# Attention's gates as tanh of half the projection, and new durations in the planner, in a two-layer kernel on one core

## The chip, the cores and the metric

The kernel runs on one core of one Trainium2 chip. The metric is the device time of one execution in microseconds (us), as the median of several runs. A separate execution was profiled; every view of the trace quoted here belongs to that one execution.

A core has five engines that run their own instruction streams in order and meet through semaphores: PE (TensorE, matrix products and transposes), DVE (VectorE), ACT (ScalarE, activation functions and copies), POOL (GpSimd) and SP, which here issues the DMA transfers. PEld in a profile is PE's loading of weights.

## The reference

Two layers work on an array `x` of 256 x 256 tokens with 128 channels, in float32. Only layer 0 matters for the change: attention along each of the 256 rows, with 4 heads of 32 channels, a mask, a bias that all rows share, and a gate.

```python
q = einsum('bnqc,hdc->bnhqd', q_x, wq) * scale
k = einsum('bnkc,hdc->bnhkd', kv_x, wk)
v = einsum('bnkc,hdc->bnhkd', kv_x, wv)
a = einsum('bnhqd,bnhkd->bnhqk', q, k) + mask_bias + triangle_bias
a = softmax(a, axis=-1)
o = einsum('bnhqk,bnhkd->bnhqd', a, v)
o = swapaxes(o, -2, -3)
g = sigmoid(einsum('bnqc,hdc->bnqhd', q_x, wg) + bg)
o = (o * g).reshape(...)
return einsum('bnqe,ce->bnqc', o, wo) + bo
...
x = x + attention(_gn(x), kv_x, ...)
x = x + layer_1(_gn(x), ...)
```

`_gn` normalises `x` by statistics over groups of channels. Layer 1 is a convolution, four selective scans over 65,536 tokens and an output product.

## The kernel before

`_layer0` works in two passes. The first reads all of `x` for its statistics. The second is attention: 64 groups of 4 rows, each row 256 tokens. `project(g)` lays out the work of a group, `row(i)` that of a row.

**No order is written by hand.** Each piece of work is a task with an engine (or a choice of two), a name in the table `COST` (L68 to L80: occupation and latency in us), a due time and the tasks that it needs. `Play` (L87) walks through model time: at each step it takes the task that can start first, and among those within `close` of it the one that is due first, and emits its instructions. Every engine then executes its stream in that order. So a number in `COST` is in no instruction, but it decides which instruction stands where, and which of two engines gets a copy.

**A group** (`project`). SP loads `xt`, `kt` and the mask `mk`. For each half `j` of the group's 1024 tokens, PE transposes four blocks of `xt` and of `kt` into PSUM (`tpx`, `tpk`); DVE normalises the first into `xn` (L62), ACT or DVE copies the second into `kvT` (L373). PE multiplies by `wq`, `wk`, `wv` (`pq`, `pk` at L451, `pv` at L475), and ACT or DVE takes the result out to `qT`, `kT`, `v`. The gate is the product `pg` (L495): two 512-column products, one for each half, held in two banks of PSUM at once until a single ACT task `sigmoid` (L506) takes out both with `AF.Sigmoid`, one instruction for each half, into `gT`.

**A row** (`row`). PE forms the scores `sp` of the four heads (L557, 16 matmuls of 32 x 128, four PSUM banks of their own), DVE adds the bias that POOL has put together (L538) and takes the row's extreme (L576, cost `soft`), ACT takes the exponential and its sum (L590, cost `exp2`, two instructions for each head), PE transposes the result (`pT`, L628), and ACT or DVE copies it out to `e` (L373). DVE inverts the sums (L610), POOL spreads them (`bc`, L615). PE then puts into one bank (`po`) two transposes of `bc` (L646) and 16 matmuls of `e` by `v` (L651, tiles of 128 x 32). DVE multiplies that by the gate and by the inverse sum (L659, L660) into `og`, PE multiplies by `wo` (`pout`, L674), and DVE adds the residual (L680). After each fourth row SP stores the group, and PE turns it (`x1p`) for the statistics of layer 1.

**PSUM** has eight banks: four for the scores, four (`banks`) for everything else. A job (`job`, L353) takes a bank when its PE work starts and gives it back when the engine that takes the result out is done.

A row's tasks are due by the row number `i`: scores at `i - 0.6`, exponentials and transposes of head `h` at `i + 0.6 + 0.2h`, `po` at `i + 1.5`, `pout` at `i + 2`. The gates' products were due at `U - 1`, with `U` the group's first row, and the sigmoid at `U - 2`.

The weights are turned once at the start (L266 to L273), each from PSUM to SBUF with an ACT copy. `vec["bg"]` holds the gate's bias as a column.

Of the kernel before, what the change touches and what calls it, by code (L numbers as in the profile page):

```python
# [8 lines left out]
F32 = mybir.dt.float32  # L9
AF = mybir.ActivationFunctionType  # L10
ALU = mybir.AluOpType
# [4 lines left out]
P = 128  # L16
N = 256
# [43 lines left out]
def _normalise(nc, out, in_, mr):  # L61
# [3 lines left out]
SEM = 0.07  # L65
# [9 lines left out]
    "turn8": (0.885, 1.05), "mm": (0.87, 1.05), "dp": (1.0, 1.15), "turn4": (0.45, 0.62),  # L75
    "turn_b": (0.67, 0.85), "dma": (0.36, 1.6), "dma2": (0.72, 3.2),
    "d512": (0.60, 0.69), "n512": (0.62, 0.81), "t256": (0.34, 0.42), "og": (0.76, 0.85),
    "soft": (0.85, 0.95), "exp2": (0.90, 1.0), "gate": (3.85, 2.60), "bias": (4.54, 4.55),
    "bc": (0.62, 0.70), "four": (0.95, 1.25), "dma3": (1.0, 1.6),
}  # L80


# [4 lines left out]
class Play:  # L87
# [14 lines left out]
    def task(self, eng, cost, due, emit, deps=(), gate=None, more=0, lag=0.0):  # L102

        t = Task()
        t.eng = (eng,) if isinstance(eng, str) else eng
        t.cost = (cost,) if isinstance(cost, str) else cost
        t.due, t.emit, t.gate, t.after, t.by = due, emit, gate, [], None
        t.ready, t.left, t.lag = 0.0, more, lag
        for d in deps:
            if d.by is None:  # L110
                d.after.append(t)
                t.left += 1
            else:
                t.ready = max(t.ready, self.after_own(d) if t.eng == (d.by,) else d.end + SEM)
        if t.left == 0:
            self.offer(t)
        return t
# [79 lines left out]
def free_after(tasks, then):  # L197
    count = Countdown(len(tasks), then)
    for t in tasks:
        on_done(t, count.one)  # L200
# [19 lines left out]
def both(*gates):  # L220
    gates = [g for g in gates if g is not None]

    def gate():
        latest = 0.0
        for g in gates:
            r = g()
            if r is None:
                return None
            latest = max(latest, r)
        return latest  # L230

    return gate


def _layer0(tc, ctx, const, ident, gmat, vec, a, x1, x1T):


    nc = tc.nc
# [3 lines left out]
    BPG = RG * NB  # L242
    W = RG * N

    keep = ctx.enter_context(tc.tile_pool(name="l0keep", bufs=1))
    wk = ctx.enter_context(tc.tile_pool(name="l0wk", bufs=1))
# [18 lines left out]
    wT = {}  # L265
    for w in ("wq", "wk", "wv", "wg", "wo"):  # L266
        raw = wk.tile([P, C], F32, tag=f"raw_{w}", name=f"raw_{w}")
        src = a[f"L0_conv_{w}"]
        nc.sync.dma_start(raw, src if w == "wo" else src.rearrange("h d c -> (h d) c"))
        pt = any_bank.tile([P, 512], F32, "m", f"pt_{w}")  # L270
        nc.tensor.transpose(pt[:, 0:P], raw, ident)
        wT[w] = keep.tile([P, P], F32, tag=w, name=f"{w}T")
        nc.scalar.copy(wT[w], pt[:, 0:P])  # L273
    bo = keep.tile([P, 1, C], F32, tag="bo", name="bo")
    nc.sync.dma_start(bo[:, 0, :], a["L0_conv_bo"].partition_broadcast(P))
    tri = keep.tile([P, NB, H, N], F32, tag="tri", name="tri")
# [7 lines left out]
    scale = 1.0 / float(CH) ** 0.5  # L284
# [99 lines left out]
    def cols(j):  # L384
        return slice(j * 512, (j + 1) * 512)
# [27 lines left out]
    def project(g):  # L413

        U = RG * g
        w = groups[g] = {
            k: Lazy(k, f"{k}_{g}")
            for k in ("xt", "kt", "mk", "xn", "kvT", "qT", "kT", "gT", "v", "x1t", "x1c")
        }

        def load(kind, src):
            def emit(t):
                nc.sync.dma_start(w[kind].get().rearrange("p (t c) -> p t c", c=C), tokens(src, g))

            return emit

        def load_mask(t):
            src = a["L0_conv_mask_bias"][0, g * RG : (g + 1) * RG, 0, 0, :]
            nc.sync.dma_start(
                w["mk"].get().rearrange("p (r k) -> p r k", k=N), src.partition_broadcast(P)  # L430
            )

        lx = sp(U - 8, load("xt", x), (), w["xt"].gate)
        lk = sp(U - 8, load("kt", kv), (), w["kt"].gate)
        w["masked"] = sp(U - 7, load_mask, (), w["mk"].gate)
        xn, kvT, q, k, v, gates = [], [], [], [], [], []
        for j in range(BPG // 4):
            xn.append(job(
                f"tpx_{g}_{j}", U - 5 + j, [("turn4", turned(lambda: w["xt"].tile, j))],
                lambda pt, by, j=j: _normalise(nc, w["xn"].tile[:, cols(j)], pt, mr0), [lx], "n512",  # L440
                "DVE", w["xn"].gate, w["xn"].get,
            ))
            kvT.append(job(
                f"tpk_{g}_{j}", U - 5 + j, [("turn4", turned(lambda: w["kt"].tile, j))],
                copy(lambda j=j: w["kvT"].tile[:, cols(j)]), [lk], gate=w["kvT"].gate,
                first=w["kvT"].get, **EITHER,
            ))
        for j in range(BPG // 4):

            def product(what, src, j=j):  # L450
                return lambda pt: nc.tensor.matmul(  # L451
                    pt, wT[what], w[src].tile[:, cols(j)], start=True, stop=True
                )

            def scaled(pt, by, j=j):
                dst = w["qT"].tile[:, cols(j)]
                if by == "ACT":
                    nc.scalar.mul(dst, pt, scale)
                else:
                    nc.vector.tensor_scalar(dst, pt, scale, None, ALU.mult)  # L460

            q.append(job(
                f"pq_{g}_{j}", U - 4.5 + j, [("mm", product("wq", "xn"))], scaled, [xn[j]],
                gate=w["qT"].gate, first=w["qT"].get, **EITHER,
            ))
            k.append(job(
                f"pk_{g}_{j}", U - 2.4 + j, [("mm", product("wk", "kvT"))],
                copy(lambda j=j: w["kT"].tile[:, cols(j)]), [kvT[j]], gate=w["kT"].gate,
                first=w["kT"].get, **EITHER,
            ))  # L470

            def values(pt, j=j):
                for i in range(4):
                    t = 4 * j + i
                    nc.tensor.matmul(  # L475
                        pt[:, i * P : (i + 1) * P], w["kvT"].tile[:, t * P : (t + 1) * P], wT["wv"],
                        start=True, stop=True,
                    )

            v.append(job(  # L480
                f"pv_{g}_{j}", U - 2 + j, [("mm", values)],
                copy(lambda j=j: w["v"].tile[:, cols(j)]), [kvT[j]], gate=w["v"].gate,
                first=w["v"].get, **EITHER,
            ))
        free_after([kvT[0], kvT[1]], w["kt"].free)
        free_after([*k, *v], w["kvT"].free)

        held_banks = {}

        def gate_of(j):  # L490
            def emit(t):
                w["gT"].get()
                at = banks.take()
                held_banks[j] = (at, ps.tile([P, 512], F32, tag=f"m{at}", name=f"pg_{g}_{j}"))
                nc.tensor.matmul(  # L495
                    held_banks[j][1], wT["wg"], w["xn"].tile[:, cols(j)], start=True, stop=True
                )

            return emit

        def two_banks():
            return banks.free[1][0] if len(banks.free) > 1 else None

        g0 = task("PE", "mm", U - 1, gate_of(0), xn, both(two_banks, w["gT"].gate))
        g1 = task("PE", "mm", U - 1, gate_of(1), [g0], banks.gate)

        def sigmoid(t):
            for j in range(BPG // 4):
                nc.scalar.activation(
                    w["gT"].tile[:, cols(j)], held_banks[j][1], AF.Sigmoid, bias=vec["bg"]  # L510
                )
                banks.give(held_banks[j][0], t.end + SEM)

        gated = task("ACT", "gate", U - 2, sigmoid, [g0, g1])
        free_after([*q, g1], w["xn"].free)

        def add_bias(t):
            xt = w["xt"].tile.rearrange("p (t c) -> p t c", c=C)
            nc.gpsimd.tensor_tensor(xt, xt, bo.to_broadcast([P, BPG, C]), ALU.add)

        biased = task("POOL", "pool", U + 0.5, add_bias, xn)
        w.update(q=q, k=k, pv=v, gated=gated, biased=biased, ends=[])
        w["row"] = {
            kind: Countdown(RG, w[kind].free) for kind in ("mk", "qT", "kT", "gT", "v", "xt")
        }

    def row(i):
# [128 lines left out]

        def gate(pt, by):
            og = z["og"].get()
            nc.vector.tensor_tensor(og, pt[:, 0:N], w["gT"].tile[:, at], ALU.mult)  # L659
            nc.vector.tensor_tensor(og, og, pt[:, N : 2 * N], ALU.mult)  # L660

        og = job(
            f"po_{i}", i + 1.5, [("four", weigh)], gate, [*leaves, bc, w["gated"], *w["pv"]], "og",
            "DVE", z["og"].gate, None,
        )
        free_after([og], z["bc"].free)
# [1307 lines left out]
```

## Time and profile before

| what | value |
|---|---|
| median of 3 runs | 24744.65 us (24725.2 to 24746.45) |
| the profiled execution | 24753.32 us |
| its span, first to last instruction | 24751.6 us |
| mean granted TensorE clock | 0.982 |
| first scores of attention (L557) | 154.26 us after the span's start |
| first scores of the last row | 2040.45 us |
| busy over the whole span | PE 93%, DVE 95%, ACT 95%, POOL 94% |

Attention's second pass fills about 154 to 2050 us; layer 1 all that follows. The shares over the whole span are therefore those of layer 1 above all. The prediction goes by windows of attention alone.

How to read the lines of a profile that follow. A line such as `L495 PE MATMUL pg<-xn,wgT` names the line of the kernel, the engine, the operation and the tiles (written <- read). In a timeline the first number is the start in us from the span's start, the second the time from the first start to the last end of the instructions merged into the line, `x4` their number, and the bracket the engine's idle time just before them with what ended it. In the list of groups the numbers after `|` are busy us in all and the mean ns of one, and then the idle time before them. Matmuls are pipelined: the next can start before the shown end, so the distance between starts tells more than the length.

### The profile page before, as it was taken

How to read it: one execution, taken by the hardware profiler on the slowest of the kernel's cores; microseconds unless marked ns; L12 is line 12 of the kernel's file. 1: busy time of each engine (PE TensorE's matmuls, PEld its weight loads, DVE VectorE, ACT ScalarE, POOL GpSimd, SP SyncE). 2: the span in 40 equal slices, each digit the busy share in tenths (PEclk: the TensorE clock that was granted, in tenths of full speed). 3: DMA queues.
4: the chain of work that ended last, by engine and by line, in shares of the span. 5: the costliest groups of instructions: out<-in, count | busy, mean ns of one | idle time of the engine just before them, and what ended most of it. 6: DMA issues, size and time to landing. Idle time of an engine off the chain costs nothing. (4 is left out here: it accounts for less than half of the span.)

```text
span 24751.6 us, 464821 instructions
## 1 busy us (share of the span) xinstructions
PE 23003.9 (93%) x165172; PEld 18188.1 (73%) x165172; DVE 23434.1 (95%) x19272; ACT 23427.6 (95%) x46416; POOL 23325.3 (94%) x17424
## 2 busy tenths in 40 slices
PE   8999999999999999999999999999998888888888
PEld 6666666666666788888887777777777777777777
DVE  7887999999999999999999999999999999999999
ACT  7998899999998999999999999999999999999998
POOL 5777999999999999999999999999999999999999
PEclk9999999999999999999999999999999999999999
DMA  4225777777777666666666777777775555555555
GB/s 131 90 90 171 255 259 264 259 260 262 261 259 255 233 233 225 232 228 229 231 230 232 243 245 243 244 243 244 244 243 198 180 184 178 181 182 181 185 178 168
DMA packets 2471853, 5355.13 MB, mean 216 GB/s; under 512 B 177121, under 2 KB 1366424, under 8 KB 2469528
## 3 DMA queue, kind: packets, MB, share of 16 engines
q1 hardware_dynamic: 2469240, 5324.34, 64.0%
q8 instruction: 1305, 21.38, 0.4%
q14 instruction: 1020, 8.36, 0.1%
q0 software_dynamic: 288, 1.05, 0.0%
HBM read 4846.54 MB, written 478.15 MB: 215 GB/s over the span
## 5 line engine op out<-in xcount | busy, mean ns | idle before, releaser
L1805 POOL TENSOR_TENSOR hc<-w,c 128x1024 f32<-128x1024 f32 x6255 | 14726.7, 2376 | 529.5 <-DVE w L1787 195.1
L1787 DVE TENSOR_TENSOR_SCAN w<-w,hst,s 128x1024 f32<-128x1024 f32 x5550 | 12670.6, 2329 | 295.0 <-PE s L1741 143.8
L1824 PE MATMUL y<-ident,hc 128*128 128x128 f32 x65536 | 8478.1, 277 | 520.8 <-ACT part L1377 204.8
L1741 PE MATMUL s<-ident,bx 128*128 128x128 f32 x57344 | 7713.6, 279 | 1020.7 <-DVE w L1787 662.0
L1741 PEld LDWEIGHTS s<-ident,bx 128*128 128x128 f32 x57344 | 6428.1, 142 | 3009.5 <-DVE w L1787 1289.0
L1335 ACT ACTIVATE bx<-dtuT,bT 128x256 f32<-128x256 f32 x19751 | 8578.3, 502 | 2.8 <-PE s L1741 2.5
L1824 PEld LDWEIGHTS y<-ident,hc 128*128 128x128 f32 x65536 | 7445.2, 142 | 1407.1 <-POOL hc L1805 598.2
L1721 ACT ACTIVATE w<-dt,negA 128x1024 f32<-128x1024 f32 x7168 | 8126.5, 1148 | 31.3 <-PE y L1824 15.8
L1337 POOL TENSOR_SCALAR bx<-dtuT,bT 128x256 f32<-128x256 f32 x8921 | 4103.7, 483 | 22.6 <-ACT dtuT L1034 5.9
L1787 DVE TENSOR_TENSOR_SCAN s<-w,hst,s 128x1024 f32<-128x1024 f32 x1618 | 3775.7, 2338 | 310.1 <-PE s L1741 205.7
L1805 DVE TENSOR_TENSOR hc<-s,c 128x1024 f32<-128x1024 f32 x1937 | 2366.2, 1223 | 101.6 <-DVE s L1787 27.5
L1762 POOL TENSOR_TENSOR w<-xu,b 128x1024 f32<-128x1024 f32 x1024 | 2423.2, 2372 | 0.5 <-issue 0.4
L1093 PE MATMUL cv<-xn,wtap 128*128 128x512 f32 x4608 | 2217.6, 600 | 5.5 <-ACT xn L1080 5.5
L1787 DVE TENSOR_TENSOR_SCAN w<-s,hst,w 128x1024 f32<-128x1024 f32 x705 | 1642.3, 2337 | 58.8 <-ACT s L1721 55.1
L538 POOL TENSOR_TENSOR bias<-tri,mk 128x2048 f32<-128x2048 f32 x256 | 1167.1, 4559 | 378.8 <-DVE nm L576 218.2
L1812 ACT COPY hst<-w 128x1 f32<-128x1 f32 x6255 | 1138.1, 185 | 276.7 <-DVE w L1787 244.7
L1721 ACT ACTIVATE s<-dt,negA 128x1024 f32<-128x1024 f32 x1024 | 1143.0, 1116 | 89.1 <-DVE hc L1805 88.1
L1093 PEld LDWEIGHTS cv<-xn,wtap 128*128 128x128 f32 x4608 | 790.1, 193 | 529.4 <-issue 523.2
L1219 PE MATMUL dp<-xd,dtw 8*128 8x512 f32 x2048 | 1169.4, 662 | 5.2 <-ACT xd L1189 0.9
L590 ACT ACTIVATE s<-s,nm 128x256 f32<-128x256 f32 x2048 | 1028.3, 515 | 0.8
L576 DVE CUSTOM_DVE_ANT_0 s<-sp,bias 128x256 f32<-128x256 f32 x2048 | 754.4, 415 | 69.1 <-PE sp L557 61.1
L1787 DVE TENSOR_TENSOR_SCAN s<-s,hst,w 128x1024 f32<-128x1024 f32 x319 | 745.2, 2336 | 67.4 <-POOL w L1762 67.4
(183 smaller groups left out, 19594.3 us busy)
## 6 DMA issues: line engine op xcount, KB each, us to landing
c<-xp_d SPq DMA_DIRECT2D x7040, 512.0 KB
b<-xp_d SPq DMA_DIRECT2D x896, 512.0 KB
yrow_d<-ys SPq DMA_DIRECT2D x128, 1024.0 KB
yl<-yrow_d SPq DMA_DIRECT2D x512, 256.0 KB
xc_d<-xu SPq DMA_DIRECT2D x128, 512.0 KB
yl<-xc_d SPq DMA_DIRECT2D x128, 512.0 KB
xu<-xc_d SPq DMA_DIRECT2D x128, 512.0 KB
xcT_d<-wtap SPq DMA_DIRECT2D x128, 512.0 KB
```

What stands on the lines that cost most here:

```text
L538: nc.gpsimd.tensor_tensor(z["bias"].get(), tri.rearrange("p b h k -> p (b h) k"), w["mk"].tile.rearrange("p (r k) -> p r k", k=N)[:, r : r ...
L1093: return lambda pc: nc.tensor.matmul(pc, wtap[:, j, t, :], xn[:, 2 * q + u : 2 * q + u + 2, v : v + N], start=t == 0, stop=t == 8,)
L1219: return lambda pt: nc.tensor.matmul(pt, dtw[:, k, j, :], xd.half[0][0:R, q * 512 : (q + 1) * 512], start=True, stop=True,)
L1335: nc.scalar.mul(dst, src, b)
L1337: nc.gpsimd.tensor_scalar(dst, src, b, 1.0, ALU.mult, ALU.mult)
L1721: nc.scalar.activation(dst, w["dt"].half[j], AF.Exp, scale=negA[:, k * ND + j, n : n + 1])
L1741: nc.tensor.transpose(dst[:, x * P : (x + 1) * P], blocks(half)[:, x, :], ident)
L1762: nc.gpsimd.tensor_tensor(box["w"].half[0], w["xu"].half[j], b_now().half[0], ALU.mult)
L1787: nc.vector.tensor_tensor_scan(rev(states), rev(a), rev(b), hst[k][:, j, n : n + 1], ALU.mult, ALU.add)
L1805: eng.tensor_tensor(box["hc"].half[0], states, c_now().half[0], ALU.mult)
L1812: nc.scalar.copy(dst, src)
L1824: nc.tensor.matmul(gr["y"][:, x, :], hc[:, x * P : (x + 1) * P], ident, is_transpose=True, start=gr["fresh"] and x == 4 * q, stop=stop and ...
```

## The change

It has three parts.

The gate is computed as `sigmoid(y) = (1 + tanh(y / 2)) / 2`: ACT forms `tanh(0.5 * pg + 0.5 * bg)` with `AF.Tanh`; the multiplication on DVE becomes `(gT + 1) * po`; the factor of one half goes into `wo`, which is halved as it is copied.

The two halves of a gate become two ordinary jobs, due at `U - 2` and `U - 1`. Each holds one bank, and its own ACT instruction takes it out (cost `a512`).

Four durations of the planner change, and `weigh` gets a name of its own, `six`, where it shared `four` with the scores.

```diff
-    "soft": (0.85, 0.95), "exp2": (0.90, 1.0), "gate": (3.85, 2.60), "bias": (4.54, 4.55),
-    "bc": (0.62, 0.70), "four": (0.95, 1.25), "dma3": (1.0, 1.6),
+    "soft": (0.69, 0.79), "exp2": (0.985, 1.09), "gate": (3.85, 2.60), "bias": (4.54, 4.55),
+    "bc": (0.62, 0.70), "four": (1.07, 1.35), "six": (1.335, 1.6), "dma3": (1.0, 1.6),
...
-        nc.scalar.copy(wT[w], pt[:, 0:P])
+        nc.scalar.mul(wT[w], pt[:, 0:P], 0.5 if w == "wo" else 1.0)
+    hbg = keep.tile([P, 1], F32, tag="hbg", name="hbg")
+    nc.scalar.mul(hbg, vec["bg"], 0.5)
...
-        held_banks = {}
-
-        def gate_of(j):
-            def emit(t):
-                w["gT"].get()
-                at = banks.take()
-                held_banks[j] = (at, ps.tile([P, 512], F32, tag=f"m{at}", name=f"pg_{g}_{j}"))
-                nc.tensor.matmul(
-                    held_banks[j][1], wT["wg"], w["xn"].tile[:, cols(j)], start=True, stop=True
-                )
-
-            return emit
-
-        def two_banks():
-            return banks.free[1][0] if len(banks.free) > 1 else None
-
-        g0 = task("PE", "mm", U - 1, gate_of(0), xn, both(two_banks, w["gT"].gate))
-        g1 = task("PE", "mm", U - 1, gate_of(1), [g0], banks.gate)
-
-        def sigmoid(t):
-            for j in range(BPG // 4):
-                nc.scalar.activation(
-                    w["gT"].tile[:, cols(j)], held_banks[j][1], AF.Sigmoid, bias=vec["bg"]
-                )
-                banks.give(held_banks[j][0], t.end + SEM)
-
-        gated = task("ACT", "gate", U - 2, sigmoid, [g0, g1])
-        free_after([*q, g1], w["xn"].free)
+        gates = [
+            job(
+                f"pg_{g}_{j}", U - 2 + j, [("mm", product("wg", "xn", j))],
+                lambda pt, by, j=j: nc.scalar.activation(
+                    w["gT"].tile[:, cols(j)], pt, AF.Tanh, bias=hbg, scale=0.5
+                ), [xn[j]], "a512", gate=w["gT"].gate, first=w["gT"].get,
+            )
+            for j in range(BPG // 4)
+        ]
+        free_after([*q, *gates], w["xn"].free)
...
         def gate(pt, by):
             og = z["og"].get()
-            nc.vector.tensor_tensor(og, pt[:, 0:N], w["gT"].tile[:, at], ALU.mult)
+            nc.vector.scalar_tensor_tensor(
+                og, w["gT"].tile[:, at], 1.0, pt[:, 0:N], ALU.add, ALU.mult
+            )
             nc.vector.tensor_tensor(og, og, pt[:, N : 2 * N], ALU.mult)
...
-            f"po_{i}", i + 1.5, [("four", weigh)], gate, [*leaves, bc, w["gated"], *w["pv"]], "og",
+            f"po_{i}", i + 1.5, [("six", weigh)], gate, [*leaves, bc, *w["gates"], *w["pv"]], "og",
```

`product` moves out of the loop over `j` and takes `j` as an argument, so that the gates can use it. Layer 1 is not touched.

More of the change, by code (lines that the diff above doesn't have):

```diff
@@ L435, in project @@
         w["masked"] = sp(U - 7, load_mask, (), w["mk"].gate)
-        xn, kvT, q, k, v, gates = [], [], [], [], [], []
+        xn, kvT, q, k, v = [], [], [], [], []
         for j in range(BPG // 4):
@@ L447, in project, with product @@
             ))
+        def product(what, src, j):
+            return lambda pt: nc.tensor.matmul(
+                pt, wT[what], w[src].tile[:, cols(j)], start=True, stop=True
+            )
         for j in range(BPG // 4):
-            def product(what, src, j=j):
-                return lambda pt: nc.tensor.matmul(
-                    pt, wT[what], w[src].tile[:, cols(j)], start=True, stop=True
-                )
             def scaled(pt, by, j=j):
@@ L462, in project @@
             q.append(job(
-                f"pq_{g}_{j}", U - 4.5 + j, [("mm", product("wq", "xn"))], scaled, [xn[j]],
+                f"pq_{g}_{j}", U - 4.5 + j, [("mm", product("wq", "xn", j))], scaled, [xn[j]],
                 gate=w["qT"].gate, first=w["qT"].get, **EITHER,
@@ L466, in project @@
             k.append(job(
-                f"pk_{g}_{j}", U - 2.4 + j, [("mm", product("wk", "kvT"))],
+                f"pk_{g}_{j}", U - 2.4 + j, [("mm", product("wk", "kvT", j))],
                 copy(lambda j=j: w["kT"].tile[:, cols(j)]), [kvT[j]], gate=w["kT"].gate,
@@ L486, in project @@
         free_after([*k, *v], w["kvT"].free)
-        held_banks = {}
-        def gate_of(j):
-            def emit(t):
-                w["gT"].get()
-                at = banks.take()
-                held_banks[j] = (at, ps.tile([P, 512], F32, tag=f"m{at}", name=f"pg_{g}_{j}"))
-                nc.tensor.matmul(
-                    held_banks[j][1], wT["wg"], w["xn"].tile[:, cols(j)], start=True, stop=True
-                )
-            return emit
-        def two_banks():
-            return banks.free[1][0] if len(banks.free) > 1 else None
-        g0 = task("PE", "mm", U - 1, gate_of(0), xn, both(two_banks, w["gT"].gate))
-        g1 = task("PE", "mm", U - 1, gate_of(1), [g0], banks.gate)
-        def sigmoid(t):
-            for j in range(BPG // 4):
-                nc.scalar.activation(
-                    w["gT"].tile[:, cols(j)], held_banks[j][1], AF.Sigmoid, bias=vec["bg"]
-                )
-                banks.give(held_banks[j][0], t.end + SEM)
-        gated = task("ACT", "gate", U - 2, sigmoid, [g0, g1])
-        free_after([*q, g1], w["xn"].free)
+        gates = [
[8 more added lines that the diff above has]
+        free_after([*q, *gates], w["xn"].free)
         def add_bias(t):
@@ L521, in project @@
         biased = task("POOL", "pool", U + 0.5, add_bias, xn)
-        w.update(q=q, k=k, pv=v, gated=gated, biased=biased, ends=[])
+        w.update(q=q, k=k, pv=v, gates=gates, biased=biased, ends=[])
         w["row"] = {
@@ L658, in gate @@
             og = z["og"].get()
-            nc.vector.tensor_tensor(og, pt[:, 0:N], w["gT"].tile[:, at], ALU.mult)
+            nc.vector.scalar_tensor_tensor(
+                og, w["gT"].tile[:, at], 1.0, pt[:, 0:N], ALU.add, ALU.mult
+            )
             nc.vector.tensor_tensor(og, og, pt[:, N : 2 * N], ALU.mult)
         og = job(
-            f"po_{i}", i + 1.5, [("four", weigh)], gate, [*leaves, bc, w["gated"], *w["pv"]], "og",
+            f"po_{i}", i + 1.5, [("six", weigh)], gate, [*leaves, bc, *w["gates"], *w["pv"]], "og",
             "DVE", z["og"].gate, None,
```

## The prediction

> **What bounds the kernel now.** I read the table by stages first, because the page's shares mix attention with the 22.7 ms of layer 1, which the change leaves alone. The lines below are a steady stretch of attention; the columns are busy us of PE, PEld, DVE, ACT, POOL, then granted clock, DMA share, GB/s.
>
> ```profile
> 400.00:600.00 200.00, 196.24 (x1824) 138.85 (x1823) 165.49 (x625) 192.70 (x576) 148.00 (x62) 1.00 0.31 93
> 600.00:800.00 200.00, 195.61 (x1814) 137.65 (x1813) 165.36 (x624) 193.81 (x591) 148.18 (x61) 1.00 0.30 91
> ```
>
> Two engines are nearly full: PE 98%, ACT 96%. DVE (83%), POOL (74%) and DMA (30%) are not. Then the groups of ACT over the whole run:
>
> ```profile
> L509 ACT ACT_TABLE_LOAD x64 | 82.1, 1283 | 1.0
> L590 ACT ACT_TABLE_LOAD x64 | 82.1, 1283 | 1.2
> ```
>
> Each of the 64 groups of four rows loads the sigmoid's table and then the exponential's again: 2 x 1.283 = 2.57 us of ACT. The timeline of ACT around one gate shows where they stand:
>
> ```profile
> 624.12 1.28 ACT L509 ACT_TABLE_LOAD   x1
> 625.41 1.26 ACT L509 ACTIVATE gT<-pg,vecs 128x512 f32<-128x512 f32 x2
> 627.66 1.07 ACT L373 COPY e<-pT 128x512 f32<-128x512 f32 x2 [0.98 <-PE pT L628]
> 628.75 1.28 ACT L590 ACT_TABLE_LOAD   x1
> ```
>
> The load before this one for L590 began at 599.11, so a group takes 29.64 us. ACT itself waits 0.98 us for PE in it. So the loads are not simply the bound; what counts is what they cost PE. The timeline of PE, from the products before the first exponential of a group:
>
> ```profile
> 599.58 1.02 PE L451 MATMUL pk<-kvT,wkT 128*128 128x512 f32 x2
> 601.06 0.33 PE L628 MATMUL pT<-ident,s 128*128 128x128 f32 x1 [0.46 <-DVE x1t L680]
> 601.56 0.55 PE L628 MATMUL pT<-ident,s 128*128 128x128 f32 x3 [0.17 <-ACT s L590]
> 601.94 1.02 PE L451 MATMUL pq<-xn,wqT 128*128 128x512 f32 x2
> 602.80 0.60 PE L628 MATMUL pT<-ident,s 128*128 128x128 f32 x4
> 603.24 1.02 PE L451 MATMUL pk<-kvT,wkT 128*128 128x512 f32 x2
> 604.19 1.15 PE L557 MATMUL sp<-kT,qT 32*128 32x256 f32 x16
> 605.27 0.44 PE L646 MATMUL po<-ident,bc 128*128 128x128 f32 x2
> 605.64 1.07 PE L651 MATMUL po<-e,v 128*32 128x256 f32 x16
> 606.64 1.53 PE L628 MATMUL pT<-ident,s 128*128 128x128 f32 x12
> ```
>
> Here I take start to start, since modelled ends overlap. A 512-column product with undisturbed followers takes 0.86 (601.94 to 602.80), four transposes 0.44 (602.80 to 603.24). So pk at 599.58 could have been followed at 600.44; the next block starts at 601.06: 0.62 lost. That block of four then takes 0.88 to 601.94 instead of 0.44: 0.44 lost. Both losses stand on the exponential that came after the table load (599.11 to 600.39, first half 600.41 to 600.92). No other PE wait stands in the timeline of this group. **PE loses 1.06 us of 29.64 per group to the loads; the other 28.58 are PE's own work.**
>
> **A rule against this reading.** The Trainium skill (Trainium Kernel Development and Optimization, Performance Expectations) holds that PE's matmul busy time says little about the distance to its limit and that LDWEIGHTS busy time is to be taken. By that PE would be at 69% (138 of 200), ACT the only bound, and taking out 2.57 us of ACT per group would give 64 x 2.57 = 164 us. By the rows, PE's blocks repeat at the same interval in every group wherever no wait is shown (0.44, 0.86, 1.08), so PE streams without room. I follow the rows: the intervals, unlike busy time, are not modelled.
>
> **PE's own work per group, from start intervals.** 16 pT and 6 tpx, tpk, x1p at 0.4365 = 9.60; 4 po at 1.312 (610.66 to 611.97) = 5.25; 4 sp at 1.077 = 4.31; 6 pq, pk, pg at 0.8605 = 5.16; 2 pv at 0.893 (608.89 to 609.78) = 1.79; 4 pout at 0.446 = 1.78. Sum 27.89. On top come changes between tiled (sp and the e-times-v part of po) and whole-array matmuls: a block ahead of sp takes +0.093 (pk 603.24 to 604.19 is 0.95); a block of transposes after sp or po +0.057 (613.04 to 613.54 is 0.50; po after sp 605.27 to 606.64 is 1.37); a product after sp +0.10 (in the ramp, pq 155.33 to 156.29 is 0.96). Before: 3 x 0.093 + 7 x 0.057 = 0.68. 27.89 + 0.68 + 1.06 = 29.63, against 29.64 measured, so nothing is missing.
>
> **The change, part by part.**
>
> *Tanh for sigmoid.* Built, the changed program has 771 table loads; the trace of before has 898 in all. So 127 go, and tanh is served beside the exponential: one load remains in attention. Per group ACT loses 2.57 us. PE loses its 1.06 us of waiting, not 2.57: what is late next is PE's own stream. The Trainium skill (ScalarE: Activation LUTs, What ACT_TABLE_LOAD costs) prices a switch at about 2.66 us, a drain included; by it 127 x 2.66 = 338 us would go. The timeline shows 1.28 per load with the next instruction 0.01 to 0.02 later (624.12, 625.41), so no drain to be saved here; on ACT it is 127 x 1.283 = 163 us.
>
> *Each half on its way out.* Two activations of 128x512 per group as before (0.63 each, 1.26 for two), now apart, each freeing its own bank of PSUM. PE's pg products are as many as before. No trace row shows tanh: at best it costs a copy's 0.47 interval, at worst, by the nearest row (sigmoid), 0.63; I take 0.63. Either way ACT has room: in the built order ACT gets 20.05 copies a group (e 12.1, k and q 2 each, kv 2, v and x1c 1 each; 18.1 before) at 0.47 = 9.4, 32 exponentials at 0.49 = 15.7, two gates 1.3: 26.4 us of a group, 2.4 under PE's stream.
>
> *Gate multiply.* (tanh + 1) times po is one DVE instruction in place of one, 128x256. The nearest row is L659, 0.42 to 0.46; a multiply-add form could take up to twice that. DVE after: 16 soft x 0.69 = 11.0, 2 xn x 0.73 = 1.5, 6 copies x 0.60 = 3.6 (7.9 before), 4 og x 0.80 = 3.2, 4 residuals x 0.34 = 1.4, 4 reciprocals x 0.12, 2 statistics x 0.61 = 1.2: 22.4. Even 4 x 0.42 more leaves it 4.8 under PE. Nothing waits but pout, which stands at least two blocks of transposes behind its po.
>
> *Halves in the weights.* wo's copy becomes a multiply, and hbg is one 128x1 instruction more, once, before the ramp: 0.2 us at most, beside DMA waits of the first 128 us. A 4-byte tile more in SBUF: no cost.
>
> *New durations for the play.* They are in no instruction, but they reorder every engine. soft 0.69, exp2 0.985, sp 1.07 and po 1.335 are what the rows show (before: 0.85, 0.90, 0.95, 0.95), so waits of the plan should be waits of the chip. In the built order a steady group again has 42 PE blocks, the same work. But sp is now followed by pv, pout, pk and pT, never by po, and preceded by pT (twice), pout and tpk; every po is followed by pT. Changes of mode: 4 x 0.093 + 5 x 0.057 + 3 x 0.10 = 0.96, or 0.28 more than before. PE's stream is then 27.89 + 0.96 = 28.85. The Trainium skill (TensorEngine Tiling (Array Packing), Key Properties) says that a change of tiling mode drains TensorE; it speaks against this order, gives no price, and the rows above give it.
>
> *New waits.* SP's loads and stores keep number and size. With PE's running sum laid against ACT's and DVE's from a group's first sp: po of the second row starts at 12.0 and needs ACT's copy of its last pT (done in PE at 11.2; copy done near 12.0, needed at 12.4 after po's own transposes); pout of the third row, at 23.0, needs the bank of v's copy, which ACT gives near 22.9 to 23.0; the first pq at 4.6 needs xn near 4.4. All fit within 0.1 to 0.4 us. I allow 0.08 us a group, with 0 and 0.6 as ends: 0.6 if two of these miss by 0.3 each, behind which the whole PE stream stands.
>
> **Sum.** Group after 28.93, before 29.64: 0.71 less. From the first sp to that of the last group there are 63 periods: 45 us. Ramp and tail have the same work; I put them at nothing, plus or minus 4. Layer 1 has the same instructions in the same order on every engine. The profiled execution took 24753.3 (span 24751.6), so 24708; that execution lies 9 us above the median of the runs, 24744.65, so the forecast is **24,700**.
>
> **Rivals.** (1) *ACT was the bound*, PE stretches: 164 us less, 24,581. For it: ACT 96%, and the waits for "ACT s" by PE. Against it: the fixed intervals. 4%. (2) *The gain is eaten by new waits* at the places above: 0.4 to 0.8 us a group, leaving 0 to 25 us: about 24,732. For it: ACT's long unbroken run before them; against it: over 2 us of room a group. 27%. (3) *Slower, by PSUM banks*: the four banks of projections. Banks now also stand open for two gates until ACT comes round. If ACT reaches each gate or v late, the next PE block waits for the bank and the rest queues behind it. From 0.79 us a group on (29.64 less 28.85) it is slower; at 1.6, 0.8 per gate, 63 x 0.81 = 51 us: 24,796. Against it: the 2.4 us of room. 8%. (4) *Tanh in another table*: four loads a group, ACT 31.5: 63 x 1.9 = 120 us more, 24,865. The 771 loads exclude it nearly: 1%. The forecast has 60%.
>
> **How the numbers follow.** This kernel's measurement can tell about 0.2%, 49 us, from no change. The forecast's own ceiling is 63 x 0.79 = 50 us plus ramp and run scatter (the runs shown span 21 us); so of its 60%, 30 fall beyond 49 us and 30 within. With (1) faster has 34%; with (2) and a little of (3) within has 59%; slower 7%. The range, 24,668 to 24,747, takes the forecast with no wait, a cheaper change of modes (0.3 us a group, 19 us) and scatter at its low end, and (2) entire at its high end; (1), (3), (4) stay out.
>
> **What would show it.** Right: period near 28.9; no table load in a group; PE's pT after pk without the 0.62 and 0.44; PE near 99%, ACT near 91%; sp followed by a block lengthened by 0.06 to 0.10. Wrong: period under 28.8 (modes cheaper), or PE waits for ACT copies, xn or banks over 0.3 us a group; a gate multiply over 0.6 us; tanh over 0.7 us.

## The result and the profile after

| what | before | after |
|---|---|---|
| median of 7 runs each | 24743.59 us (24725.2 to 24751.1) | 24664.08 us (24656.99 to 24679.78) |
| span of the profiled execution | 24751.6 us | 24662.3 us |
| period of a group in attention | 29.64 us | 28.90 us |
| ACT's table loads in all | 898 | 771 |

The ratio of the times is 0.997, with a 95% interval of 0.9959 to 0.998: 79.5 us less. That is 34.5 us more than the 45 us forecast, 4 us below the low end of the range, and on the far side of 0.2%, where the prediction put its smaller chance.

The traces can be cut at four marks: the start of the first scores, the start of the last row's scores, the first scan of layer 1, and the end. The second column spans 255 rows.

| trace | to the first scores | first to last scores | to the first scan | layer 1 from there |
|---|---|---|---|---|
| before | 154.3 | 1886.2 | 100.0 | 22611.1 |
| after | 139.9 | 1832.7 | 102.2 | 22587.5 |
| difference | -14.4 | -53.5 | +2.2 | -23.6 |

The four sum to the 89.3 us between the two spans. Attention's share is 8.5 us above the forecast. The first column was forecast at nothing. Layer 1 has the same instructions in the same order; its share is taken up below.

The steady stretch of attention after, in the table by stages (columns as before: busy us of PE, PEld, DVE, ACT, POOL, then clock, DMA share, GB/s):

```profile
400.00:600.00 200.00, 200.00 (x1852) 142.61 (x1854) 160.60 (x628) 186.70 (x594) 151.41 (x64) 1.00 0.31 93
600.00:800.00 200.00, 200.00 (x1864) 142.94 (x1864) 159.87 (x621) 186.89 (x596) 153.82 (x63) 1.00 0.31 93
```

PE is covered without a gap, ACT has come down from 96% to 93%, DVE from 83% to 80%. The waits of the same stretch, longest first (who waited, for whom, us in total, times, longest):

```profile
POOL bias L523 <- DVE nm L561: 210.6, 152, 2.7
DVE s L561 <- PE sp L542: 127.3, 167, 1.5
POOL bias L523 <- PE pT L613: 121.6, 55, 2.5
ACT e L375 <- PE pT L613: 96.8, 111, 1.3
```

Before, the same list had two waits of PE's matmuls:

```profile
PE pT L628 <- ACT s L590: 20.0, 78, 0.5
PE pT L628 <- DVE x1t L680: 13.9, 30, 0.5
```

Now it has none; the other engines wait, mostly for PE. The timeline of PE shows what a group consists of:

```profile
602.30 0.60 PE L613 MATMUL pT<-ident,s 128*128 128x128 f32 x4
602.83 1.15 PE L542 MATMUL sp<-kT,qT 32*128 32x256 f32 x16
603.90 0.71 PE L661 MATMUL pout<-woT,og 128*128 128x128 f32 x4
604.45 0.60 PE L613 MATMUL pT<-ident,s 128*128 128x128 f32 x4
...
609.41 1.15 PE L542 MATMUL sp<-kT,qT 32*128 32x256 f32 x16
610.48 1.12 PE L452 MATMUL pk<-kvT,wkT 128*128 128x512 f32 x2
611.45 0.38 PE L631 MATMUL po<-ident,bc 128*128 128x128 f32 x2
...
622.53 1.15 PE L542 MATMUL sp<-kT,qT 32*128 32x256 f32 x16
623.61 1.16 PE L478 MATMUL pv<-wvT,kvT 128*128 128x128 f32 x8
624.60 1.02 PE L452 MATMUL pg<-xn,wgT 128*128 128x512 f32 x2
```

From start to start: the pT ahead of sp takes 0.53 in place of 0.44, pout after sp 0.55 in place of 0.45, pk after sp 0.97 in place of 0.86, pv after sp 0.99 in place of 0.89. They agree with the surcharges of 0.093 and 0.10 in the prediction's sum.

The costs of the two altered instructions, in the list of groups (busy us in all, mean ns of one, idle time before them). First before, then after for 300 to 1900 us:

```profile
L509 ACT ACTIVATE gT<-pg,vecs 128x512 f32<-128x512 f32 x128 | 81.0, 684 | 0.8
L659 DVE TENSOR_TENSOR og<-po,gT 128x256 f32<-128x256 f32 x216 | 90.8, 420 | 88.3 <-PE po L651 88.3
```

```profile
L494 ACT ACTIVATE gT<-pg,hbg 128x512 f32<-128x512 f32 x111 | 76.6, 690 | 3.7
L644 DVE SCALAR_TENSOR_TENSOR og<-gT,po 128x256 f32<-128x256 f32 x221 | 92.5, 418 | 74.3 <-PE po L636 74.3
```

Tanh takes 690 ns where the sigmoid took 684, and add-and-multiply 418 where the multiply took 420. Neither form costs anything that matters here.

### The profile page after: what moved, and what is told of

Read it like the earlier page. It is cut to its first block, busy times and chain, and to the rows that moved or that the text cites. A ratio compares the mean times of both kernels' runs of the same rounds, so it can differ in the third digit from the quotient of the medians.

```text
span 24662.3 us, 463909 instructions
## 1 busy us (share of the span) xinstructions
PE 22976.3 (93%) x165172; PEld 18190.0 (74%) x165172; DVE 23350.1 (95%) x19150; ACT 23324.4 (95%) x46412; POOL 23322.3 (95%) x17424
```

## The experiments

Every kernel was timed against the kernel before on the same chip. A period is the distance between the first scores of successive groups.

### Is the shorter statistics pass a matter of place?

The statistics pass has the same instructions on PE and DVE in the same order, but its loads of `x` came faster. The table by stages for that pass, first of before, then of after (last column: GB/s):

```profile
20.00:40.00 20.00, 11.51 (x88) 9.23 (x87) 13.32 (x21) 0.00 (x0) 0.00 (x0) 1.00 1.20 290
40.00:60.00 20.00, 11.74 (x89) 9.41 (x88) 14.66 (x24) 0.00 (x0) 0.00 (x0) 1.00 1.17 288
```

```profile
20.00:40.00 20.00, 13.25 (x101) 10.54 (x100) 16.44 (x26) 0.00 (x0) 0.00 (x0) 1.00 1.11 331
40.00:60.00 20.00, 12.87 (x98) 10.37 (x99) 15.60 (x25) 0.00 (x0) 0.00 (x0) 1.00 1.09 327
```

The 128x1 tile `hbg` takes 32 bytes of each partition in the layout, and everything behind it in layer 0 moves up. The first `xs` tile lies at byte 62688 before, an odd multiple of 32, and at 62720 after, a multiple of 64; the other `xs` tiles follow 4096 bytes apart. Two kernels tell place from chance.

**The tile alone** (before, with an unused tile where `hbg` would be):

```diff
+    pad = keep.tile([P, 1], F32, tag="pad", name="pad")
+    nc.scalar.mul(pad, vec["bg"], 0.5)
     bo = keep.tile([P, 1, C], F32, tag="bo", name="bo")
```

> The kernel before with one unused 128x1 tile at the place where the change puts hbg, so that the tiles behind it in SBUF move by 32 bytes, from an odd multiple of 32 to a multiple of 64. Theory A (the faster statistics pass of the profile after comes from where the tiles lie): the pass ends near 112 us instead of 126, the loads of x come each 1.51 us instead of 1.80, attention's period stays at 29.64, and the time falls by about 14 us. Rival B (chance of that execution): the pass ends near 126 us and the time is that of before.

**The change with the tiles at their old remainders:**

```diff
-    hbg = keep.tile([P, 1], F32, tag="hbg", name="hbg")
+    hbg = keep.tile([P, 16], F32, tag="hbg", name="hbg")[:, 0:1]
```

> The changed kernel with hbg's tile 64 bytes wide, so that the tiles behind it lie at odd multiples of 32 bytes again. Theory A: the statistics pass takes 126 us again, loads of x 1.80 us each, attention's period stays at 28.90, and of the 80 us gained some 65 remain: about 24,680. Rival B: the pass keeps to either value by chance, and the time stays near 24,664.

Measured: the tile alone 24714.76 us, ratio 0.9991 (0.9982 to 1.0001); the change with the tiles back 24678.87 us, ratio 0.9978 (0.9968 to 0.9987), 14.8 us above the changed kernel. The same stretches of the pass, of the first and of the second kernel:

```profile
20.00:40.00 20.00, 13.61 (x104) 10.87 (x102) 16.32 (x26) 0.00 (x0) 0.00 (x0) 1.00 1.12 334
40.00:60.00 20.00, 13.47 (x103) 11.01 (x104) 16.36 (x27) 0.00 (x0) 0.00 (x0) 1.00 1.13 338
```

```profile
20.00:40.00 20.00, 11.56 (x88) 9.42 (x88) 13.71 (x22) 0.00 (x0) 0.00 (x0) 1.00 1.15 288
40.00:60.00 20.00, 11.85 (x90) 9.42 (x88) 14.55 (x23) 0.00 (x0) 0.00 (x0) 1.00 1.14 290
```

The rate follows the place in both directions: 334 to 338 GB/s with `xs` at multiples of 64, 288 to 290 at odd multiples of 32. In all ten traces of this study the median distance of two loads was 1.50 or 1.51 us with the one and 1.80 with the other. Chance is out. Which multiple is needed is open: 62720 is also a multiple of 128 and of 256, and the slow places (62688, and 62752 in the second kernel) are multiples of none of the three. Attention's period is 29.64 with the tile alone and 28.90 with the tiles back, so place does nothing to the period. The first kernel's median lies 21.6 us under that of before, with an interval that reaches past no change; its trace puts 16.5 us of it at the place, with the first scores at 137.8 us in place of 154.3.

### Which part of the change gives the period?

**Tanh and the two jobs, without the new durations:**

```diff
-    "soft": (0.69, 0.79), "exp2": (0.985, 1.09), ...
-    ... "four": (1.07, 1.35), "six": (1.335, 1.6), ...
+    "soft": (0.85, 0.95), "exp2": (0.90, 1.0), ...
+    ... "four": (0.95, 1.25), "six": (0.95, 1.25), ...
```

> The change without its new durations: tanh, two jobs for the gates, but soft, exp2, four and six as before (six 0.95). Theory P (PE's stream bounds a group once the table loads are gone): no table load in a group, PE over 98% busy, period 28.5 to 29.1, most of the 0.74 us a group. Rival D (it is the new durations that make it, since the old ones place ACT's work too early): PE waits for ACT again, period over 29.3.

Measured: 24675.21 us, ratio 0.9977 (0.9967 to 0.9986); period 29.12. That is 0.52 of the 0.74 us a group, so theory P holds in kind, though 29.12 misses the upper end of its 28.5 to 29.1. PE is 99.4% busy, with one marked wait in a group, for the gate's activation (0.16 us; from start to start the place loses 0.32, as pout ahead of it began at 617.12):

```profile
617.89 0.66 PE L613 MATMUL pT<-ident,s 128*128 128x128 f32 x4 [0.16 <-ACT gT L494]
```

**The new durations, without tanh:** before, with the four numbers of the diff, `six` for `weigh`, and the unused tile.

```diff
-    "soft": (0.85, 0.95), "exp2": (0.90, 1.0), ...
-    ... "four": (0.95, 1.25), ...
+    "soft": (0.69, 0.79), "exp2": (0.985, 1.09), ...
+    ... "four": (1.07, 1.35), "six": (1.335, 1.6), ...
...
-            f"po_{i}", i + 1.5, [("four", weigh)], gate, ...
+            f"po_{i}", i + 1.5, [("six", weigh)], gate, ...
```

> The new durations without tanh: one sigmoid task for both gates with its two table loads, plus the same unused tile as in the run with the tile alone. Theory P: the loads take ACT 2.57 us of a group; ACT then has 26.4 + 2.6 = 29.0 against PE's 28.6 to 28.9, so the period is 29.0 to 29.6 and at most half of the 0.74 us comes. Rival D: the durations are what mattered, period 28.9 as in the changed kernel.

Measured: 24749.7 us, ratio 1.0007 (0.9998 to 1.0017), although its statistics pass has the faster loads. Both theories missed: the groups alternate between 29.44 and 31.20 us, 30.32 in the mean, 0.68 longer than before. All marked waits of PE in two such groups, from its timeline:

```profile
600.42 0.66 PE L630 MATMUL pT<-ident,s 128*128 128x128 f32 x4 [1.19 <-ACT e L375]
620.77 0.41 PE L648 MATMUL po<-ident,bc 128*128 128x128 f32 x2 [0.85 <-DVE e L375]
661.06 0.66 PE L630 MATMUL pT<-ident,s 128*128 128x128 f32 x4 [1.19 <-ACT e L375]
```

The first and third are the same place two groups apart (60.64 us). PE waits 2.04 us in that time for copies of `e`: pT for one that frees a bank, po for one that it multiplies (and that frees a bank too). ACT is 97% busy (193.80 of 200 us) with its table loads still in. Part of the longer group is not waiting: counted in this timeline with the prediction's surcharges, changes between tiled and whole-array matmuls come to 0.94 us a group, where they were 0.68. So truer durations on four entries did not by themselves make a better order. With the sigmoid's block still in, the order that they gave is worse, and only together with tanh do they bring their 0.22 us. Why the planner falls into that order I did not trace further.

### Is PE's stream really what a group lasts?

**One product more on PE.** The first gate product of a group is formed twice into the same bank (`twice` calls its product two times):

```diff
...
-                f"pg_{g}_{j}", U - 2 + j, [("mm", product("wg", "xn", j))],
+                f"pg_{g}_{j}", U - 2 + j, [("mm", twice(product("wg", "xn", j)) if j == 0 else product("wg", "xn", j))],
```

> The changed kernel with the first gate product of each group formed twice into the same bank: one 512-column product (0.861 us) more on PE in a group, nothing on any other engine. Theory P (a group lasts as long as PE's stream): period 28.90 + 0.86 = 29.76, 64 x 0.86 = 55 us more in all, about 24,720. Rival L (ACT or a loop of waits sets the period and PE follows): less than half of that.

Measured: 24717.4 us, ratio 0.9991 (0.9981 to 1.0); period 29.76. The whole 0.86 us arrives, while ACT has more room than in the changed kernel (92% in place of 93%, in the table by stages):

```profile
400.00:600.00 200.00, 200.00 (x1823) 141.50 (x1821) 155.41 (x605) 183.39 (x582) 148.92 (x61) 1.00 0.29 88
```

**Two copies more on ACT:**

```diff
+        def squash(pt, j):
+            dst = w["gT"].tile[:, cols(j)]
+            nc.scalar.copy(dst, pt)
+            nc.scalar.activation(dst, pt, AF.Tanh, bias=hbg, scale=0.5)
...
+                lambda pt, by, j=j: squash(pt, j), [xn[j]], "a512", ...
```

> The changed kernel with a plain copy of each gate's bank ahead of its tanh: two 128x512 copies (0.47 us each) more on ACT in a group, PE as it was. Theory P: ACT had 2 us of a group to spare, so the period stays within 28.90 to 29.0 and the time within 6 us. Rival L (ACT's chain sets the period): 0.94 us a group more, 60 us in all.

Measured: 24689.64 us, ratio 0.9979 (0.997 to 0.9988); period 29.19. Neither number was met: of 0.94 us on ACT, 0.29 came through, with ACT at 95 to 96%. The timeline of PE shows the larger piece:

```profile
604.20 0.61 PE L664 MATMUL pout<-woT,og 128*128 128x128 f32 x4
604.89 0.66 PE L616 MATMUL pT<-ident,s 128*128 128x128 f32 x4
```

After pout the next block stands 0.69 us later in place of 0.446: 0.24 lost, once in every group. In the list of waits for 300 to 1900 us stands a wait of PE's weight loads, once in a group, that the changed kernel does not have:

```profile
PEld pT L616 <- ACT gT L494: 14.6, 55, 0.3
```

Here the gate's tanh ends at 604.84, 0.05 before that block starts: the block stands behind a gate that holds its bank longer. ACT's spare time is real on average (over 2 us a group), but at the gates the slack is a few tenths. An engine with room still delays PE when work lands on it at a place that the planner did not know of.

### Does layer 1 gain from the same placement?

A 32-byte tile ahead of layer 1's pool:

```diff
     p1 = ctx.enter_context(tc.tile_pool(name="l1p1", bufs=1))
+    nc.vector.memset(p1.tile([P, 8], F32, tag="pad", name="pad"), 0.0)
```

> The changed kernel with a 32-byte tile ahead of layer 1's pool, so that all of layer 1's tiles lie at multiples of 64 bytes too. If the placement speeds loads as in the statistics pass (1.80 to 1.51 us for 512 KB), each of layer 1's 7,936 loads of b and c takes about 0.3 us less. Theory H (these loads are hidden behind the scan's engines): layer 1 stays within its scatter of 22,580 to 22,611 us. Rival E (the loads set part of layer 1's pace): 50 us less or more.

Measured: 24678.43 us, ratio 0.9975 (0.9965 to 0.9985); layer 1 took 22604.1 us from its first scan. No gain, so rival E is out. If anything layer 1 was slower: 16.6 us more than in the trace of the changed kernel, and the median of the time lies 14 us above that kernel's, which was timed in another session. Whether the move did that was not traced. Theory H's range holds; that these loads are hidden is its reading and was not shown by itself. Over the ten traces layer 1 took 22579.5 to 22611.1 us; but for the moved tiles here, its instructions are the same in all of them. The kernel before happened to be profiled at the top of that scatter: its profiled execution (24753.32 us) lies 10 us above the median of its 7 runs and 17 above that of 31 later ones. So 10 to 17 of the 23.6 us in the table above belong to that one execution, and what makes layer 1 scatter was not studied.

### A better order

If PE's stream is the bound and changes between tiled and whole-array matmuls are the part of it that an order can save, a planner that knows them should gain. Core of the edit, with due times of most tasks shifted as well:

```diff
+    def change(self, c):
+
+        tiled = self.last in ("four", "six")
+        if c == "four":
+            return 0.0 if self.last == "six" else 0.093
+        return (0.1 if c == "mm" else 0.057) if tiled else 0.0
...
+            if self.modes and e == "PE" and self.last == "six":
+                r, t = min(
+                    ((r, t) for r, t in can if t.cost[0] == "four" and r <= first + self.hold),
+                    key=lambda x: x[0], default=(r, t),
+                )
...
+    play.cost = dict(COST, turn4=(0.437, 0.62), six=(1.312, 1.6), mm=(0.866, 1.05), four=(1.077, 1.35), a512=(0.625, 0.78))
```

> The changed kernel with a planner for attention that knows what a change between tiled and whole-array matmuls costs PE, takes scores right behind a po where it can, and has due times chosen for that order. Changes of mode in a group come to 0.25 us instead of 0.96. Theory P: period 27.89 + 0.25 = 28.14, up to 28.3 with small waits; about 45 us less than the changed kernel, 24,620. Rival L: other waits fill the place, period 28.7 or more, no gain that can be told.

Measured: 24613.88 us (4 runs), ratio 0.9948 (0.9933 to 0.9963): 123 us less than before, 50 less than the changed kernel's median. Period 28.13, where theory P had 28.14. The timeline of PE, at the seam:

```profile
607.49 1.07 PE L659 MATMUL po<-e,v 128*32 128x256 f32 x16
608.49 1.15 PE L565 MATMUL sp<-kT,qT 32*128 32x256 f32 x16
609.57 1.09 PE L636 MATMUL pT<-ident,s 128*128 128x128 f32 x8
610.50 1.02 PE L475 MATMUL pk<-kvT,wkT 128*128 128x512 f32 x2
```

Scores follow po directly, 1.00 after the start of its tiled part, with no surcharge on either side; only the first block behind them is longer (eight transposes 0.93 in place of 0.87). The table by stages shows how far this goes:

```profile
400.00:600.00 200.00, 200.00 (x1901) 146.25 (x1903) 152.72 (x624) 199.87 (x633) 156.89 (x66) 1.00 0.32 96
```

PE has no gap, and ACT is covered as well; which of the two would bind next, this trace does not tell.

All cuts side by side (us):

| kernel | period | to first scores | first to last scores | layer 1 |
|---|---|---|---|---|
| before | 29.64 | 154.3 | 1886.2 | 22611.1 |
| after | 28.90 | 139.9 | 1832.7 | 22587.5 |
| tile alone | 29.64 | 137.8 | 1884.8 | 22597.7 |
| tiles back | 28.90 | 154.3 | 1832.9 | 22590.8 |
| tanh alone | 29.12 | 137.6 | 1849.4 | 22579.5 |
| durations alone | 30.32 | 139.9 | 1917.9 | 22589.9 |
| PE + 0.86 | 29.76 | 142.0 | 1886.7 | 22586.7 |
| ACT + 0.94 | 29.19 | 141.3 | 1853.4 | 22590.4 |
| layer 1 moved | 28.90 | 138.6 | 1832.7 | 22604.1 |
| paired | 28.13 | 137.6 | 1781.5 | 22602.8 |

## Why the prediction was right in its mechanism and short in its size

**What bounds attention.** Right. PE gave back its waits behind a table load, and no more. (The prediction put the first of them, 0.46 in its bracket, down to the exponential, where the row names DVE's `x1t`. In the trace the first exponential ended at 600.92, 0.15 before that start, as the second one did before the next transposes; `x1t` ended at 601.07, at the start itself. The row alone does not decide between them; without table loads neither wait is there.) Rival 1, by which ACT's whole 2.57 us a group would go, is excluded by the period. The rule quoted in the prediction from the Trainium skill (Trainium Kernel Development and Optimization, Performance Expectations), which takes LDWEIGHTS busy time as the measure, would still show ample room (71% after); adding 0.86 us to PE and getting 0.86 us back shows that there is none.

**The sum for a group.** Right: 28.93 forecast, 28.90 measured. Its terms hold one by one in the timeline: 0.09 ahead of sp, 0.10 for a product behind it. The wait allowed for was 0.08 us; what is left over the 28.85 of the stream is 0.05. The 28.85 was counted in the order as built, so what the trace confirms are its prices and that so little waiting was added.

**Tanh, the gate multiply, the freed halves.** Right: no table load in a group, 690 and 418 ns. ACT's share was put at 91% and came out at 93%.

**"A 4-byte tile more in SBUF: no cost."** This is the step that failed. The tile costs nothing where it stands, but the layout gives it 32 bytes, and that moved the statistics pass's `xs` tiles to multiples of 64. It gave 14 us: the first scores came 14.4 earlier. The medians of 1.80 and 1.51 us would give 18.6 for 64 loads; the mean distances, 1.82 and 1.60, give the 14. A gain can come from an edit that has no work in it.

**"Ramp and tail have the same work; I put them at nothing, plus or minus 4."** Too small. First to last scores fell by 53.5 where 63 periods give 63 x 0.74 = 46.6. The first four groups took 106.7 us in place of 114.6, of which the steady difference explains 3.0; the way from the last scores to layer 1 gave 2.2 back. All that is not steady was thus worth 4.7 us, where the prediction had nothing, plus or minus 4; what shortened the start was not traced.

**The forecast of the time.** 14.4 for the statistics pass, 53.5 for attention less 2.2 behind it make 65.7 us that belong to the change. The medians show 79.5 in the first comparison; against the kernel before's median of 24736.31 (31 runs, beside the later kernels) it is 72, and the kernel with the tiles back, timed beside those 31, lies 57 below it, which with the 14.4 makes 72 again. What is left over 65.7 is within the scatter of layer 1, and whether some of it belongs to the change stays open; a miss of the range by 4 us can be scatter too. The chances followed from the too small terms: a "ceiling of 50 us" was right for the steady groups and wrong for the kernel.

**The rivals.** New waits (2) ate at most 0.05 us a group, not 0.4 to 0.8. Banks (3) did not make it slower, but they are where it is sensitive: the run with more ACT work lost 0.24 us a group just there. Another table for tanh (4) is excluded by the 771 loads, of which attention has one.

## What to carry to other kernels

When one engine's stream is continuous, cost an edit by what it takes off that stream and not by what it takes off the engine it edits: 2.57 us of ACT were worth 1.06 us of PE, less the 0.28 us of mode changes that the new order brought. Take the stream from start-to-start intervals, context by context; here they gave the periods of the changed and the paired order to 0.05 us, and an order chosen to avoid the surcharges in them was worth another 50 us. Before calling an edit free because it has no instruction in the loop, ask what else it moves: tile addresses, and with them the rate of loads in a stage that is bound by them.

## What was not expected of the hardware

A stream of 512 KB loads from HBM into SBUF ran at 288 to 290 GB/s into tiles at odd multiples of 32 bytes (two traces) and at 313 to 338 GB/s into tiles at multiples of 64 (eight traces), in the stretches from 20 to 60 us; the median distance of two loads was 1.80 against 1.50 or 1.51 us. The boundary itself may be 64, 128 or 256 bytes. In layer 1, moving the tiles in the same way brought no gain.

Changes between tiled and whole-array matmuls cost PE 0.06 to 0.10 us each, but scores directly behind the tiled part of po cost nothing more (1.00 us from start to start).
